# A soft mixture of experts inside a fused kernel: four places for the dispatch weights, the fourth part's maxima earlier, phi loaded by blocks

## The chip, the cores and the metric

The kernel runs on one core of a Trainium2 chip. The time is the device time of that core in microseconds for one run of the whole program; the median over runs is compared. The profile is one execution recorded by the hardware profiler; its times are counted from the start of its span.

## What is computed

The program is a chain of four blocks of attention and feed-forward layers on 16 sequences of 256 tokens with 128 features. The change lies in the feed-forward layer of the second block, a soft mixture of 64 experts with 32 slots each:

```
def _L1_ffn_ref(x, phi, W, b):            # x (16, 256, 128), phi (128, 64, 32), W (64, 128, 128)
    logits = einsum('bmd,dnp->bmnp', x, phi)
    dispatch = softmax(logits, axis=0)     # over the 16 sequences
    combine = softmax(logits.reshape(b, m, n * p), axis=-1)   # over the 2048 slots
    slots = einsum('bmd,bmnp->bnpd', x, dispatch)
    y = einsum('bnpd,nde->bnpe', slots, W) + b[None, :, None, :]
    out = einsum('bnpd,bmnp->bmd', y, combine)
...
x = x + layernorm(_L1_ffn_ref(layernorm(x), ...))
```

The dispatch weights are normalised over the sequences, so each needs the maximum and the sum over all 16 of them; the combine weights are normalised over the slots, which the kernel does with a running maximum.

## The kernel before

The work of the layer is in `stage_soft_moe`. The 2048 slots are cut into eight blocks of 256 slots. For block n three generators are woven together, step by step: `share(n)`, `logits(n + 2)` and `slots(n + 1)`. So a block of the loop finishes the outputs of one block of slots, computes the slot inputs and experts of the next, and the logits of the one after.

- `logits(n)` multiplies, for each of 16 batches b, the transposed tokens by 256 columns of `phi` (L1078) into a bank of `ps_s`. ScalarE copies the bank to `lg` (L1079) and VectorE reduces its maximum into `mpart` (L1080). At the end come the new running maximum and the factors `mfade` and `mless` (L1084 to L1090).
- `slots(n)` works in four parts (c, t): two groups c of 128 slots and two halves t of the 256 tokens. They are called first (0,0), second (0,1), third (1,0) and fourth (1,1). `maxima(c, t)` takes the maximum of `lg` over the 16 sequences (L1101 to L1104), subtracts it (L1105) and has ScalarE take the exponential (L1106), in a tile `mdisp` of 8 KB per partition. `weights(c, t)` sums over the sequences (L1111 to L1115), inverts (L1117) and multiplies (L1118). `inputs(c, half)` multiplies tokens and dispatch weights for eight sequences, into the two `ps_mm` banks, copied to `slT` (L1130); it needs both parts t of its c. `experts(c, half, slT)` adds biases and multiplies by the expert weights `mw`, and ScalarE copies the result to `y`, tile `my` (L1150).
- `share(n)` takes, batch by batch, the exponential of `lg` (L1199), transposes it on TensorE (L1204) into `ps_t`, has it copied to `meT` (L1206), multiplies by `y` into `ps_o`, adds that on VectorE into `x` with the factor `mfade` (L1215; a copy, L1217, for n = 0) and copies the sums of weights to `mgot` on ScalarE (L1218).

`mdisp` has three places that are taken in turn. A part's maxima can start only when the part three before it has been read by `inputs`. `slT` has three places too, and serves `inputs`, the early norm in `late` and the reloaded rows `back` in `end`. PSUM has two banks each for `ps_mm`, `ps_s`, `ps_o` and `ps_t`.

Nothing in this stage is ordered by hand beyond the steps of the generators: the framework's scheduler reorders the instructions of each engine when it builds the program, and each engine then runs its queue in that fixed order. Loads are issued from SP. `phi`, 8 KB per partition, is loaded whole with the tile `quarter` in the pool `soft` at the start of the program (L2009), and its transfer is issued at 40.5 us.

Of the kernel before, what the change touches and what calls it, by code (L numbers as in the profile page):

```python
# [21 lines left out]
F32 = mybir.dt.float32  # L22
# [7 lines left out]
NB, SEQ, P, D = 16, 256, 128, 128  # L30
NG, NT, GT = 8, 4, 512
# [160 lines left out]
def bc(ap, axis, n):  # L192

    ap = ap.unsqueeze(axis)
    shape = list(ap.shape)
    shape[axis] = n
    return ap.to_broadcast(shape)
# [826 lines left out]
def stage_soft_moe(k, x, w, wdram, bdram, xn, xs, fill):  # L1024
# [3 lines left out]

    nc, v = k.nc, k.nc.vector
    ident = k.c["ident"]  # L1030
    phi = w["phi"]
    blocks, bs = 8, 2 * P
    sums = k.t([P, 2, NB], "sums", 1)
    xT = {}
    tile_of = lambda b, t: (b // 2, 2 * (b % 2) + t)
# [3 lines left out]
    y = k.t([P, 2, NB, D + 1], "my", 1)  # L1039
# [4 lines left out]
    quarter = k.t([P, P], "mquarter", 1, dt=BF16)  # L1044
# [3 lines left out]
    def biases():  # L1048


        left = k.t([P, 16 * D], "mdisp", 3)
        nc.gpsimd.memset(left, 0.0)
        for i in range(3):
            nc.sync.dma_start(out=left[32 * i : 32 * i + 4, :], in_=bdram)
        nc.gpsimd.tensor_copy(bias, left)
        for i in (1, 2):
            for at in (slice(32, 64), slice(64, P))[i - 1 :]:
                nc.gpsimd.tensor_tensor(left[at, :], left[at, :], bias[at, :], ALU.subtract)
                nc.gpsimd.tensor_copy(bias[at, :], left[at, :])

    def late(g):

        y = k.t([P, NT, D], "slT", 3)
        yield from k.norm_to(y, xn[g])
        nc.gpsimd.tensor_tensor(x[g], x[g], y, ALU.add)
        yield
        yield from fill(g)

    def logits(n):
        lg = lgs[n % 2]  # L1070
        part = k.t([P, 2, NB], "mpart", 2)
        for b in range(NB):
            if n == 0 and b % 2 == 0:
                xT[b // 2] = k.transposed(xn[b // 2], f"mxT{b // 2}", 1)
            ps = k.ps("s").rearrange("p (t n) -> p t n", t=2)
            for t in range(2):
                g, at = tile_of(b, t)
                k.mm(ps[:, t, :], xT[g][:, at * P : (at + 1) * P], phi[:, n * bs : (n + 1) * bs])  # L1078
            nc.scalar.copy(lg[:, :, b, :], ps)  # L1079
            v.tensor_reduce(part[:, :, b], ps, AX.X, ALU.max)  # L1080
            yield

        new = k.t([P, 2, NB], "mtop", 4)
        v.tensor_tensor(new, top[-1], part, ALU.max)  # L1084
        f = fade[n] = k.t([P, 2, NB], "mfade", 3)
        v.tensor_tensor(f, top[-1], new, ALU.subtract)
        nc.scalar.activation(f, f, AF.Exp)
        top.append(new)
        less[n] = k.t([P, 2, NB], "mless", 3)
        v.tensor_scalar(less[n], new, -1.0, None, ALU.mult)  # L1090

    def slots(n):

        lg = lgs[n % 2]
        disp, rest = {}, []

        def maxima(c, t):
            src = lg[:, t, :, c * P : (c + 1) * P]
            e = disp[c, t] = k.t([P, NB, P], "mdisp", 3)
            m = k.t([P, P], "mm", 1)  # L1100
            v.tensor_tensor(e[:, 0:8, :], src[:, 0:8, :], src[:, 8:16, :], ALU.max)  # L1101
            v.tensor_tensor(e[:, 0:4, :], e[:, 0:4, :], e[:, 4:8, :], ALU.max)
            v.tensor_tensor(e[:, 0:2, :], e[:, 0:2, :], e[:, 2:4, :], ALU.max)
            v.tensor_tensor(m, e[:, 0, :], e[:, 1, :], ALU.max)  # L1104
            v.tensor_tensor(e, src, bc(m, 1, NB), ALU.subtract)  # L1105
            nc.scalar.activation(e, e, AF.Exp)  # L1106

        def weights(c, t):
            e = disp[c, t]
            s = k.t([P, 4, P], "msum", 1)  # L1110
            v.tensor_tensor(s, e[:, 0:4, :], e[:, 4:8, :], ALU.add)  # L1111
            for i in (8, 12):
                v.tensor_tensor(s, s, e[:, i : i + 4, :], ALU.add)
            for i in (2, 1):
                v.tensor_tensor(s[:, 0:i, :], s[:, 0:i, :], s[:, i : 2 * i, :], ALU.add)  # L1115
            r = k.t([P, P], "mrec", 1)
            v.reciprocal(r, s[:, 0, :])  # L1117
            v.tensor_tensor(e, e, bc(r, 1, NB), ALU.mult)  # L1118

        def inputs(c, half):  # L1120

            out = k.t([P, 8, P], "slT", 3)
            for q in range(2):
                ps = k.ps("mm").rearrange("p (b n) -> p b n", b=4)
                for i in range(4):
                    b = 8 * half + 4 * q + i
                    for t in range(2):
                        g, at = tile_of(b, t)
                        k.mm(ps[:, i, :], xn[g][:, at, :], disp[c, t][:, b, :], t == 0, t == 1)
                nc.scalar.copy(out[:, 4 * q : 4 * q + 4, :], ps)  # L1130
            return out

        def experts(c, half, slT):

            pss = [k.ps("mm") for _ in range(2)]
            at = (2 * n + c) * D
            for ps in pss:
                k.mm(ps, quarter, bc(bias[:, at : at + D], 1, 4), True, False)
            for q, ps in enumerate(pss):
                for i in range(4):  # L1140
                    for e in range(4):
                        k.mm(
                            ps[32 * e : 32 * e + 32, i * P : (i + 1) * P],
                            slT[:, 4 * q + i, 32 * e : 32 * e + 32],
                            wc[c][:, e, :],
                            False,
                            True,
                        )
                b = 8 * half + 4 * q
                nc.scalar.copy(y[:, c, b : b + 4, 0:D], ps.rearrange("p (b n) -> p b n", b=4))  # L1150

        wc = []
        for c in range(2):
            at = 2 * n + c
            wc.append(k.t([P, 4, D], "mw", 2))
            nc.sync.dma_start(out=wc[c].rearrange("p n d -> p (n d)"), in_=wdram[:, at * 512 : (at + 1) * 512])
        maxima(0, 0)
        yield
        maxima(0, 1)
        yield  # L1160
        weights(0, 0)
        yield
        maxima(1, 0)
        yield
        weights(0, 1)
        yield
        yield
        yield
        a = inputs(0, 0)
        yield  # L1170
        b = inputs(0, 1)
        yield
        weights(1, 0)
        yield
        maxima(1, 1)
        yield
        experts(0, 0, a)
        yield
        weights(1, 1)
        yield  # L1180
        yield
        a = inputs(1, 0)
        yield
        experts(1, 0, a)
        yield
        experts(0, 1, b)
        yield
        b = inputs(1, 1)
        yield
        experts(1, 1, b)  # L1190
# [37 lines left out]
    def end(g, f, got):  # L1228


        bs = slice(2 * g, 2 * g + 2)
        r = k.t([P, 2, 2], "mend", 3)
        v.tensor_tensor(r, sums[:, :, bs], f[:, :, bs], ALU.mult)
        v.tensor_tensor(r, r, got[:, :, bs], ALU.add)
        rt = k.over[g] if g in k.over else k.t([P, NT], "mendt", 3)
        v.reciprocal(rt.rearrange("p (b t) -> p t b", b=2), r)
        if g in k.over:
            return
        back = k.t([P, NT, D], "slT", 3)
        yield from soft_end(k, x[g], xs[:, g], rt, back)  # L1240
        yield
        if g == 0:
            k.stats_nb(x[g], k.kept)
# [691 lines left out]
def program(ctx: ExitStack, tc: tile.TileContext, xin, dram, at, out):  # L1935
    nc = tc.nc
# [4 lines left out]
    def opened(name, side):  # L1941
        weights[name] = pool(name, side)
        return weights[name].__enter__()
# [4 lines left out]
    def load(p, name, only=None, dt=F32):  # L1948

        got = {}  # L1950
        for n, (a, width) in at[name].items():
            if only is not None and n not in only:
                continue
            src = dram[name][:, a : a + width]
            t = p.tile([src.shape[0], width], dt, tag=f"{name}_{n}", name=f"{name}_{n}")
            nc.sync.dma_start(out=t, in_=src)
            got[n] = t
        return got
# [20 lines left out]
    k = Ctx(tc, const, None, None)  # L1979
# [26 lines left out]
    closed("w0")  # L2006
    l2 = load(opened("wb", "right"), "l2")
    psoft = opened("soft", "right")
    l1f = load(psoft, "l1f")  # L2009
    xs, xn, fill = soft_inputs(k, x, psoft)  # L2010
    stage("l1a", "left", stage_l1_attn, l1, rows1, z, fill, xn, *hand, banks=RING_BANKS)
    closed("z")
    closed("wa")

    stage("l1f", "left", stage_soft_moe, l1f, dram["l1fw"], dram["l1fb"], xn, xs, fill)
    closed("soft")
    pe = opened("we", "right")
# [50 lines left out]
```

## Time and profile before

| | |
|---|---|
| three runs | 2961.12, 2963.91 and 2964.82 us; median 2963.91 |
| the profiled execution | 2960.44 us, of which its span is 2958.7 |
| TensorE clock granted | 0.968 over the span |
| the layer | about 945 to 1535 us |
| `sums` updates (L1223, L1226) | 1099.8, 1165.28, 1230.52, 1295.76 ... 1482.3 |
| matmuls on phi columns (x512) | 141.8 us busy |
| matmuls of `meT` and `my` (x1024) | 144.1 us busy |
| matmuls of `mdisp` and `mxn` (x1024) | 125.3 us busy |
| L1105, L1118 (x32 each) | 73.1 us busy each, 2284 and 2286 ns |
| L1106 (x32) | 61.2 us busy, 1913 ns |

Busy times of one group merge the overlap of matmuls in flight, so the spacing of starts in the timeline is the better measure of what a group costs. A matmul of 32-bit floats counts as two instructions in the profile. In a line of the timeline, the first number is the start, the second the length, and `[1.98 <-ACT mdisp L1106]` says that the engine sat idle for 1.98 us until that instruction of another engine ended. A line of the table of windows gives the window, its length, and for TensorE, its weight loads, VectorE, ScalarE and POOL the busy time and the number of instructions.

### The profile page before, as it was taken

Reading aid. Unit: us, or ns where it says so; the run is one execution under the profiler, and the core shown is the slowest. Engines: PE = TensorE matmul, PEld = TensorE weight load, DVE = VectorE, ACT = ScalarE, POOL = GpSimd, SP = SyncE. Lnnn points to the kernel's source line nnn. Section 1 sums busy time; section 2 is a strip of 40 time slices with the busy share of each in tenths; the row PEclk is TensorE's granted clock in tenths of the full one; section 3 lists DMA queues with packets and bytes.
Section 4 is the critical chain, followed back from the end, with each engine's and each line's share of the span. In section 5 each row is a group of like instructions: output and inputs, shape, how many; then the busy total and the mean of one; then the engine's idle time right before and its main releaser. Section 6 shows DMA issues by size and latency. Waiting matters only on the chain.

```text
span 2958.7 us, 59454 instructions
## 1 busy us (share of the span) xinstructions
PE 2757.9 (93%) x23674; PEld 1878.8 (63%) x23674; DVE 1931.3 (65%) x5302; ACT 1676.9 (57%) x3530; POOL 1017.2 (34%) x1407
## 2 busy tenths in 40 slices
PE   8989999999998799999988998799999799978998
PEld 4556776777766588888863443566666444436897
DVE  5677466565666889999967765666574587735442
ACT  6745656455465676777735666444434377756543
POOL 3553333333336200000044555423221466644332
PEclk9989999999999899999988999899999899998999
DMA  4000000000001000000020000000000000010000
GB/s 116 12 1 2 1 2 2 1 2 1 2 2 38 1 12 12 8 9 8 9 71 5 1 1 1 1 1 1 1 1 1 1 1 1 1 51 7 2 16 16
DMA packets 29150, 31.30 MB, mean 11 GB/s; under 512 B 7292, under 2 KB 20156, under 8 KB 28732
## 3 DMA queue, kind: packets, MB, share of 16 engines
q1 hardware_dynamic: 28872, 27.49, 3.1%
q8 instruction: 187, 3.06, 0.4%
q14 instruction: 91, 0.75, 0.1%
HBM read 23.29 MB, written 4.19 MB: 9 GB/s over the span
## 4 chain that ended last, share of the span: by engine, by line
PE 50%; ACT 7%; DVE 7%; POOL 2%; issue 2%; DMA 0%; POOLq 0%; SPq 0%; ACTq 0%; DVEq 0%
PE ps_s L336 31%; PE ps_o L336 7%; PE ps_mm L336 6%; ACT at_e L491 1%; PE ps_s L325 1%; ACT lg L1199 1%; PE ps_xin L336 1%; ACT meT L1206 1%; PE ps_sum L336 1%; ACT mdisp L1106 1%; ACT lg L1079 1%; PE ps_t L1204 1%; DVE at_nm L459 1%; PE ps_s L525 1%; DVE scan L1488 1%
## 5 line engine op out<-in xcount | busy, mean ns | idle before, releaser
L459 DVE TENSOR_REDUCE at_nm<-ps_s 128x2 f32<-128x512 f32 (+1 forms) x384 | 238.1, 682 | 119.7 <-PE ps_s L336 119.7
L491 ACT ACTIVATE at_e<-ps_s 128x512 f32<-128x512 f32 x384 | 198.2, 603 | 96.7 <-PE ps_s L336 94.6
L1488 DVE TENSOR_TENSOR scan<-ps_s,lm 128x384 f32<-128x384 f32 x256 | 124.7, 549 | 142.4 <-PE ps_s L336 142.2
L497 POOL TENSOR_SCALAR_AFFINE_SELECT at_e<-at_e 128x1024 f32<-128x1024 f32 (+1 forms) x96 | 135.1, 1408 | 208.1 <-ACT at_e L491 207.8
L245 POOL TENSOR_TENSOR ln_rs<-ln_rs,mhalf 128x4 f32<-128x4 f32 x192 | 196.6, 1024 | 15.2
L1015 POOL TENSOR_TENSOR ln_rs<-ln_mv,mendt 128x4 f32<-128x4 f32 x6 | 1.2, 199 | 521.2 <-DVE ln_mv L1013 521.2
L891 DVE TENSOR_REDUCE l_max<-ps_s 128x3 f32<-128x384 f32 x256 | 124.1, 548 | 61.5 <-PE ps_s L336 61.5
L336 PE MATMUL ps_o<-my,meT 128*128 128x129 f32 x1024 | 144.1, 288 | 20.8 <-ACT mgot L1218 16.5
L336 PEld LDWEIGHTS ps_s<-l_w,mlp_h 128*128 128x128 f32 x1280 | 149.7, 192 | 20.3 <-issue 15.1
L336 PE MATMUL ps_s<-l1f_phi,mxT 128*128 128x256 f32 x512 | 141.8, 401 | 21.5 <-DVE mpart L1080 15.7
L244 POOL TENSOR_SCALAR ln_rs<-ln_mv 128x4 f32<-128x4 f32 x184 | 38.5, 209 | 338.0 <-DVE ln_mv L257 317.3
L336 PEld LDWEIGHTS ps_o<-my,meT 128*128 128x128 f32 x1024 | 127.8, 195 | 39.3 <-ACT mgot L1218 22.2
L336 PE MATMUL ps_s<-l_w,mlp_h 128*128 128x128 f32 x1280 | 151.0, 275 | 1.3 <-ACT mlp_h L824 0.9
L336 PE MATMUL ps_s<-qm,kT 32*128 32x512 f32 x768 | 144.4, 650 | 8.0 <-DVE at_nm L459 7.8
L336 PE MATMUL ps_s<-km,qT 32*128 32x512 f32 x768 | 138.4, 666 | 8.7 <-DVE qT L1632 3.7
L941 POOL TENSOR_SCALAR_AFFINE_SELECT e<-e 128x512 f32<-128x512 f32 x128 | 78.6, 635 | 172.8 <-ACT e L938 172.8
L336 PE MATMUL ps_o<-at_e,at_vm 128*32 128x128 f32 (+1 forms) x2048 | 122.7, 336 | 15.3 <-ACT at_oT L521 15.3
L336 PE MATMUL ps_mm<-mdisp,mxn 128*128 128x128 f32 x1024 | 125.3, 279 | 5.0 <-DVE mdisp L1118 4.9
L938 ACT ACTIVATE e<-ps_s 128x384 f32<-128x384 f32 x256 | 105.4, 510 | 39.4 <-PE ps_s L336 39.4
L1465 ACT COPY BT<-ps_s 128x512 f32<-128x512 f32 x64 | 37.6, 587 | 158.0 <-PE ps_s L336 158.0
L336 PEld LDWEIGHTS ps_mm<-mdisp,mxn 128*128 128x128 f32 x1024 | 121.8, 195 | 7.9 <-DVE mdisp L1118 6.6
L336 PEld LDWEIGHTS <-b_ident 128*128 128x128 bf16 x656 | 51.9, 99 | 113.1 <-issue 102.5
(462 smaller groups left out, 7203.1 us busy)
## 6 DMA issues: line engine op xcount, KB each, us to landing
mw<-in_l1fw SPq DMA_DIRECT2D x16, 256.0 KB, 2.6
moe_w<-in_moe SPq DMA_DIRECT2D x16, 256.0 KB, 5.4
l_w<-in_l SPq DMA_DIRECT2D x10, 256.0 KB, 3.3
x<-in_x SPq DMA_DIRECT2D x8, 256.0 KB, 5.8
xs<-x SPq DMA_DIRECT2D x8, 256.0 KB, 2.1
out<-x SPq DMA_DIRECT2D x8, 256.0 KB, 2.5
slT<-xs SPq DMA_DIRECT2D x6, 256.0 KB, 2.7
l1f_phi<-in_l1f SPq DMA_DIRECT2D x1, 1024.0 KB, 5.0
```

What stands on the lines that cost most here:

```text
L244: g.tensor_scalar(out, in_, scale, eps, ALU.mult, ALU.add)
L245: g.tensor_tensor(out, out, self.mhalf[:, :n], ALU.pow)
L325: self.nc.tensor.transpose(out[:n, k * P : (k + 1) * P], src[:, k, cols], self.c["ident"])
L336: self.nc.tensor.matmul(out, lhsT=lhsT, rhs=rhs, start=start, stop=stop, skip_group_check=True)
L459: v_.tensor_reduce(nm[:, t, r, vs], s, AX.X, ALU.max, negate=True)
L491: nc.scalar.activation(e[:, r], s, AF.Exp)
L497: nc.gpsimd.affine_select(at, at, [[0, 4], [0, n], [1, P]], ALU.is_ge, 0.0, base=0, channel_multiplier=-1)
L891: v.tensor_reduce(mx[:, b, :, h, 16], s, AX.X, ALU.max, negate=True)
L938: nc.scalar.activation(e[:, h].rearrange("p j n -> p (j n)"), s[:, : 3 * P], AF.Exp)
L941: nc.gpsimd.affine_select(e[:, :, j, :], e[:, :, j, :], [[0, 4], [1, P]], ALU.is_ge, 0.0, base=0, channel_multiplier=-1)
L1465: nc.scalar.copy(s, ps)
L1488: v.tensor_tensor(m, s[:, : SEQ + P], lm[:, SCAN_HEADS[4 * (t // 2) + 2 * i + hh], :], ALU.mult)
```

## The change

`mdisp` gets four places, so every part takes the place that the same part of the previous block has left. `slT` gets two. In `slots`, the step `maxima(1, 1)` moves from behind `weights(1, 0)` to the step after `weights(0, 1)`, ahead of `inputs(0, 0)`. `phi` is no longer loaded whole: the first 256 columns are loaded at the start into `phi0`, and `logits(n)` issues on SP the load of the 256 columns for `logits(n + 1)` into `mphi`, which has two places. The pool on the right side shrinks by 7 KB per partition and the work pool on the left grows by 6 KB.

```
-    phi = w["phi"]
+    phis = [w["phi0"]]
...
-        left = k.t([P, 16 * D], "mdisp", 3)
+        left = k.t([P, 16 * D], "mdisp", 4)
...
-        y = k.t([P, NT, D], "slT", 3)
+        y = k.t([P, NT, D], "slT", 2)
...
     def logits(n):
         lg = lgs[n % 2]
+        phi = phis[n]
+        if n + 1 < blocks:
+            phis.append(k.t([P, bs], "mphi", 2))
+            nc.sync.dma_start(out=phis[-1], in_=w["phi"][:, (n + 1) * bs : (n + 2) * bs])
...
-                k.mm(ps[:, t, :], xT[g][:, at * P : (at + 1) * P], phi[:, n * bs : (n + 1) * bs])
+                k.mm(ps[:, t, :], xT[g][:, at * P : (at + 1) * P], phi)
...
-            e = disp[c, t] = k.t([P, NB, P], "mdisp", 3)
+            e = disp[c, t] = k.t([P, NB, P], "mdisp", 4)
...
-            out = k.t([P, 8, P], "slT", 3)
+            out = k.t([P, 8, P], "slT", 2)
...
         weights(0, 1)
         yield
+        maxima(1, 1)
         yield
         yield
         a = inputs(0, 0)
         yield
         b = inputs(0, 1)
         yield
         weights(1, 0)
-        yield
-        maxima(1, 1)
         yield
         experts(0, 0, a)
...
-        back = k.t([P, NT, D], "slT", 3)
+        back = k.t([P, NT, D], "slT", 2)
...
-    l1f = load(psoft, "l1f")
+    l1f = load(psoft, "l1f", {"quarter"})
+    a, width = at["l1f"]["phi"]
+    l1f["phi"] = dram["l1f"][:, a : a + width]
+    l1f["phi0"] = psoft.tile([P, 2 * P], F32, tag="phi0", name="phi0")
+    nc.sync.dma_start(out=l1f["phi0"], in_=l1f["phi"][:, : 2 * P])
```

In the instruction order of the changed kernel only this stage differs. From block n=2 to n=5 the order repeats, as it does before. There VectorE starts each block with the maxima of the first and second part interleaved, then the third's; it runs L1101 to L1103 of the fourth part between the steps of the second part's weights, ahead of that part's L1118. TensorE issues `inputs(1, 0)` and `experts(1, 0)` ahead of batch 15's products on `y`, and after them `experts(0, 1)`, `inputs(1, 1)` and `experts(1, 1)`. Before, all of these but the first four matmuls of `inputs(1, 0)` come after batch 15.

## The prediction

> **What bounds the kernel now.** I read the page's busy shares first, then the table of windows over the soft mixture (945 to 1540 us), then the timelines of VectorE and TensorE through one repeating block of it.
>
> ```profile
> PE 2757.9 (93%) x23674; PEld 1878.8 (63%) x23674; DVE 1931.3 (65%) x5302; ACT 1676.9 (57%) x3530; POOL 1017.2 (34%) x1407
> ```
> ```profile
> 1165.00:1230.50 65.50, 63.29 (x652) 55.41 (x652) 59.67 (x101) 47.89 (x104) 0.00 (x0) 1.00 0.03 9
> 1230.50:1296.00 65.50, 63.30 (x653) 55.41 (x652) 59.92 (x103) 47.90 (x103) 0.00 (x0) 1.00 0.03 10
> ```
> The last shows one block: TensorE 63.3 us busy of 65.5, VectorE 59.9, ScalarE 47.9. TensorE is the bound, with VectorE close behind. The line of `sums` (L1226) starts at 1165.28, 1230.52 and 1295.76, so a block takes 65.24 us; blocks n=1 to 5 repeat one order.
>
> VectorE in that block (start, duration, what it waited for):
> ```profile
> 1230.63 1.22 DVE L1101 TENSOR_TENSOR mdisp<-lg 128x1024 f32<-128x1024 f32 x1
> ...
> 1237.81 0.69 DVE L1111 TENSOR_TENSOR msum<-mdisp 128x512 f32<-128x512 f32 x1 [1.98 <-ACT mdisp L1106]
> ...
> 1264.43 2.28 DVE L1118 TENSOR_TENSOR mdisp<-mdisp,mrec 128x2048 f32<-128x2048 f32 x1
> ...
> 1276.93 1.22 DVE L1101 TENSOR_TENSOR mdisp<-lg 128x1024 f32<-128x1024 f32 x1
> ...
> 1291.36 2.29 DVE L1118 TENSOR_TENSOR mdisp<-mdisp,mrec 128x2048 f32<-128x2048 f32 x1
> ...
> 1295.87 1.22 DVE L1101 TENSOR_TENSOR mdisp<-lg 128x1024 f32<-128x1024 f32 x1
> ```
> First part's maxima; the wait for its exponential; the second part's weights, ready at 1266.71; the fourth part's maxima; its weights; the next block. TensorE:
> ```profile
> 1260.08 0.66 PE L1204 MATMUL ps_t<-const_ident,lg 128*128 128x128 f32 x4 [0.29 <-ACT meT L1206]
> 1261.94 2.05 PE L336 MATMUL ps_o<-my,meT 128*128 128x129 f32 x16 [1.21 <-ACT mgot L1218]
> ...
> 1267.46 3.29 PE L336 MATMUL ps_mm<-mdisp,mxn 128*128 128x128 f32 x28
> ...
> 1280.30 0.59 PE L336 MATMUL ps_mm<-mbias,mquarter 128*128 128x512 bf16 x2
> ...
> 1291.42 1.16 PE L336 MATMUL ps_o<-my,meT 128*128 128x129 f32 x8
> ```
> `inputs(0,0)` needs parts one and two; TensorE reaches it at 1267.46, 0.75 us after they are ready, without waiting. So VectorE's road to the second part's weights and TensorE's other work are nearly balanced. That balance is what the change disturbs.
>
> [...] The 1.98 us wait agrees in part: it repeats, but on VectorE, since the second part's place is still held by the previous block. [...] in the trace every block of n=2 to 5 runs the same fixed order, whatever waits. [...]
> ```profile
> 1036.29 5.02 PE L336 MATMUL ps_mm<-mdisp,mxn 128*128 128x128 f32 x28 [3.46 <-DVE mdisp L1118]
> ```
> Next start 1041.15, so 28 matmuls took 4.86 us; at 1267.46 as many took 3.13.
>
> **The change, part by part.** No arithmetic is added or removed: TensorE, VectorE and ScalarE issue the same instructions in a new order, within the soft mixture alone; POOL does nothing in these blocks.
>
> *Costs at nothing.* The 1024 KB phi load becomes eight of 128 KB. A 256 KB `mw` load lands in 2.6 us; each piece has a whole 65 us block. On SP it sits beside the two `mw` loads, and its place was freed when the block before last finished. If the first piece is late, logits(1) starts late: at most about 3 us, more likely 0, since 30 us lie between. `slT` with two places: the third `back` load waits for the first final add (1504.0 plus 1.3 us, 2.7 to land: 1508), needed at about 1515; cover 7 us, cost 0, else up to 6. The layout of memory moves by some KB; at the stage's edges I allow 2 us either way.
>
> *The steady block.* Count from T, the end of batch 15's `ps_o` products, the point where VectorE's queue turns to the next block.
>
> Before: T is 1227.18. The second part is ready at 1266.71, T+39.5, and from there to the next T (1292.42) is 25.7. Sum 65.2.
>
> After, in the instruction order of the changed kernel, VectorE's work from the turn to the second part's L1118, by start-to-start times of this trace: maxima of parts one to three, 3 x 4.48 (1.14+0.60+0.34+0.20+2.20) = 13.4; fourth part's L1101 to L1103, now ahead, 2.1; two sets of weights, 2 x 5.41 (3 x 0.60+0.34+0.20+0.87+2.20) = 10.8; six L1080 x 0.60 = 3.6; six batches of L1215 x 0.52 = 3.1; small ones 0.4. Sum 33.4. The turn comes 1.0 after T (before 3.5: VectorE still had fourth-part weights then). It waits 0.8 on TensorE around batches 2 and 3 (0 to 1.9). Ready at T+35.2: **4.3 earlier**. The 1.98 wait goes, since parts one and two now start together.
>
> But from there the road is longer. The rest of the fourth part's maxima follow at once (0.20+0.26+2.20), then its exponential on ScalarE (1.9), which stands ahead of `mgot` of batch 6, whose bank batch 8's products need: 4.9 us in all against 3.1 us of `inputs(0,0)` matmuls. A new stall of 1.7. Then TensorE's queue to the next T: eight batches of `ps_o` products 7.3; eight phi products 8 x 0.87 = 7.0; `inputs(0,1)` and `inputs(1,0)` 2 x 3.57 = 7.1; `experts(0,0)` and `experts(1,0)` 2 x 2.41 (1280.30 to 1282.71) = 4.8; four sets of transposes 1.8. Sum 28.0. Before, most of `inputs(1,0)` and `experts(1,0)`, 6 us, lay after T, where they filled TensorE while VectorE prepared the second part. Now they lie before T; after T only `experts(0,1)`, `inputs(1,1)` and `experts(1,1)` are left, 8.8. So TensorE comes to `inputs(0,0)` at about T+31.5 and waits about 3.8 for the weights.
>
> Block: 35.2+4.9+28.0 = 68.1, so +2.9, taken as **+3.0**; between +2.0 (no VectorE wait: 34.4) and +5.4 (its waits at 1.9, `experts` at the 2.84 of 1242.55 to 1245.40, and a few tenths for PSUM banks). Five blocks: **+15** (10 to 27).
>
> *Start.* The fourth part no longer waits for `inputs(0,0)` to free a place, so its weights end at about 1029 where they end at 1036. But logits(1)'s last reductions fall behind, with phi(15) at 1037.8 after `inputs(1,0)` and `experts(1,0)`. That is block 0's T. Its T+68 ends at 1105.5, against 1096.85 now: **+8.6** (4 to 12).
>
> *Last slots block (n=6), no logits.* Second part ready at about T+32; 4.4 through the exponential; 22.2 of TensorE work; 1.5 wait for the fourth part's weights: 60, against 56.2 now (1422.9 to 1479.1): **+3.8** (0 to 6).
>
> *End.* All `y` are ready about 8 us after the last T where they take 17.4 (1479.1 to 1496.5): **-9.5** (-11 to -6). After that the ends of the batches run as before.
>
> Sum: 8.6+15+3.8-9.5 = **+17.9**. Against the profiled run (2960.4, span 2958.7 and 1.7 around it) that is 2978.3; the median of the runs is 3.5 above, so 2982. About 0.2%, 6 us, is what a measurement here can tell from no change.
>
> **Rivals.**
> 1. *The fourth place pays (faster).* TensorE's block is 13.9 of phi, 15.8 of `ps_o` products with their turnover, 7.0 of transposes, 14.3 of `inputs` and 11.4 of `experts`: 62.4, so 2.8 of it is waiting. If VectorE is ready by the time TensorE arrives at `inputs(0,0)`, no new wait comes and the old ones may go: 6 blocks x 2.8 = -17, and the start's 7 us earlier weights are kept in part: about 2945. For it: the 1.98 wait, and the 2.45 and 0.78 waits in the first block. Against: the moved 6 us. It decides if the second part is ready before T+31. Chance 0.19.
> 2. *It cancels.* The end's gain of 9.5 against blocks at only +1: 2964. Chance 0.11.
> 3. *The clock drops too.* The new 3.8 us wait before `inputs(0,0)` slows the 28 matmuls behind it as at 1036.29: 1.7 x 6 = +10 more, 2992. For: the line above. Against: that stretch was also sparse before the wait. Chance 0.20.
> 4. *The forecast.* 2982, its own range 2970 to 2993. Chance 0.50.
>
> That the change misses its aim is in the forecast: it sets the fourth part's maxima ahead of the third's weights, but they also come ahead of the second's last multiply.
>
> **How the numbers follow.** Slower: 4 and 3, 0.70; same 0.11; faster 0.19. Range 2957 to 3003: from the weak end of rival 1 to rival 3 with blocks at +4.
>
> **What would show it.** Right: L1226 about 68 us apart; a wait of 3 to 4 us on DVE L1118 before each `inputs(0,0)`; one of 1 to 2 us on ACT `mgot` after it; no 1.98 us wait at the block's start; VectorE's idle up by 3. Wrong: blocks at 65 or less with no L1118 wait. L1118's release under T+32 would sink the main step; waits on DMA or at the stage's edges the ones at nothing.

## The result and the profile after

The change makes the kernel slower by a little: 2981.11 us (median of four runs, 2979.37 to 2981.66) against 2962.51 (2958.86 to 2964.82), a ratio of 1.0064 with a 95% interval of 1.0051 to 1.0077. That lies 0.9 us from the forecast of 2982. The profiled execution took 2981.66 us, its span is 2979.9.

The page's busy line, the first one to read:

```profile
PE 2761.3 (93%) x23674; PEld 1888.3 (63%) x23674; DVE 1925.6 (65%) x5302; ACT 1675.7 (56%) x3530; POOL 1016.7 (34%) x1407
```

The instruction counts are those of before, and busy times moved by at most 6 us (9.5 for the weight loads). So the 21 us between the two profiled executions (spans of 2979.9 and 2958.7 us) are idle time and slower matmuls, not work. The table of windows over two blocks of the layer (window, length, then busy time of TensorE, weight loads, VectorE, ScalarE, POOL; TensorE's clock; DMA):

```profile
1236.17:1304.42 68.25, 63.73 (x651) 56.25 (x650) 58.98 (x102) 47.47 (x101) 0.00 (x0) 0.97 0.04 11
1304.42:1372.66 68.24, 63.72 (x651) 56.24 (x650) 58.97 (x101) 47.47 (x101) 0.00 (x0) 0.97 0.04 11
```

A block takes 68.25 us instead of 65.24. TensorE's clock in it was 1.00 and is now 0.97. VectorE's idle time per block rose from 5.6 us (65.24 less 59.67) to 9.3. The timeline says where. VectorE in one block:

```profile
1236.17 0.69 DVE L1084 TENSOR_REDUCE mpart<-ps_s 128x2 f32<-128x512 f32 x1 [3.51 <-ACT lg L1083]
...
1240.96 0.69 DVE L1084 TENSOR_REDUCE mpart<-ps_s 128x2 f32<-128x512 f32 x1 [3.59 <-ACT lg L1083]
...
1242.18 1.22 DVE L1105 TENSOR_TENSOR mdisp<-lg 128x1024 f32<-128x1024 f32 x1
...
1270.77 1.21 DVE L1105 TENSOR_TENSOR mdisp<-lg 128x1024 f32<-128x1024 f32 x1
...
1273.85 2.27 DVE L1122 TENSOR_TENSOR mdisp<-mdisp,mrec 128x2048 f32<-128x2048 f32 x1
...
1276.50 2.27 DVE L1109 TENSOR_TENSOR mdisp<-lg,mm 128x2048 f32<-128x2048 f32 x1
```

The first two lines are idle time just ahead of the block's turn: VectorE has 7.1 us with nothing to do, because the last two batches' products on phi, which ScalarE copies to `lg` and VectorE reduces (L1084), stand behind `inputs(1,0)` and `experts(1,0)` in TensorE's queue. Then the maxima start (1242.18), the fourth part's come in between (1270.77), and the second part's weights end at 1276.12. TensorE and ScalarE in the same block:

```profile
1240.17 1.16 PE L336 MATMUL ps_o<-my,meT 128*128 128x129 f32 x8
...
1276.17 5.02 PE L336 MATMUL ps_mm<-mdisp,mxn 128*128 128x128 f32 x28 [3.16 <-DVE mdisp L1122]
1281.03 1.06 PE L336 MATMUL ps_o<-my,meT 128*128 128x129 f32 x8
...
1308.42 1.16 PE L336 MATMUL ps_o<-my,meT 128*128 128x129 f32 x8
```
```profile
1278.81 1.91 ACT L1110 ACTIVATE mdisp<-mdisp 128x2048 f32<-128x2048 f32 x1 [1.58 <-DVE mdisp L1109]
1280.62 0.20 ACT L1221 COPY mgot<-ps_o 128x2 f32<-128x2 f32 x2
```

TensorE waits 3.16 us for the weights. Then 28 matmuls take 4.86 us (start of the first to 1281.03), where before they took 3.13. The exponential and `mgot`, which the next `ps_o` products also need, are done at about 1280.8, at nearly the same moment.

### The profile page after: what moved, and what is told of

Read it like the earlier page. It is cut to its first block, busy times and chain, and to the rows that moved or that the text cites. A ratio compares the mean times of both kernels' runs of the same rounds, so it can differ in the third digit from the quotient of the medians.

```text
span 2979.9 us, 59519 instructions
## 1 busy us (share of the span) xinstructions
PE 2761.3 (93%) x23674; PEld 1888.3 (63%) x23674; DVE 1925.6 (65%) x5302; ACT 1675.7 (56%) x3530; POOL 1016.7 (34%) x1407
## 3 DMA queue, kind: packets, MB, share of 16 engines
q8 instruction: 187, 3.06, 0.4%
## 4 chain that ended last, share of the span: by engine, by line
PE 51%; DVE 10%; ACT 4%; POOL 2%; issue 1%; POOLq 0%; ACTq 0%; DVEq 0%
PE ps_s L336 31%; PE ps_o L336 7%; PE ps_mm L336 7%; ACT at_e L491 1%; PE ps_s L325 1%; DVE mdisp L1122 1%; PE ps_xin L336 1%; PE ps_sum L336 1%; DVE mdisp L1109 1%; PE ps_t L1207 1%; DVE mpart L1084 1%; DVE at_nm L459 1%; PE ps_s L525 1%; DVE mdisp L1105 1%; DVE scan L1491 1%
## 5 line engine op out<-in xcount | busy, mean ns | idle before, releaser
L336 PE MATMUL ps_mm<-mdisp,mxn 128*128 128x128 f32 x1024 | 138.5, 297 | 28.3 <-DVE mdisp L1122 28.3
L336 PEld LDWEIGHTS ps_mm<-mdisp,mxn 128*128 128x128 f32 x1024 | 133.6, 211 | 33.2 <-DVE mdisp L1122 30.9
L336 PE MATMUL ps_s<-mphi,mxT 128*128 128x256 f32 x448 | 122.3, 396 | 19.7 <-DVE mpart L1084 19.4
L1084 DVE TENSOR_REDUCE mpart<-ps_s 128x2 f32<-128x512 f32 x128 | 87.3, 683 | 67.0 <-ACT lg L1083 66.8
```

Source lines behind the costliest of these rows:

```text
L336: self.nc.tensor.matmul(out, lhsT=lhsT, rhs=rhs, start=start, stop=stop, skip_group_check=True)
```

## Experiments

The main theory: the layer's order alone makes the difference, through two waits, TensorE's on the second part's weights and VectorE's on the last batches. The rivals: the loads and the smaller `slT`, the four places as such, and the clock. The change consists of four separable things: loads with two `slT` places, the fourth `mdisp` place, the maxima ahead, and a step that goes out of `slots` (one `yield` fewer behind `weights(1, 0)`, so all from `experts(0,0)` on comes a step earlier).

All edits are shown against the changed kernel, unless another is named.

**loads_only.** Three places and the old steps, with the new loads and two places for `slT`:
```
-        left = k.t([P, 16 * D], "mdisp", 4)
+        left = k.t([P, 16 * D], "mdisp", 3)
...
-            e = disp[c, t] = k.t([P, NB, P], "mdisp", 4)
+            e = disp[c, t] = k.t([P, NB, P], "mdisp", 3)
...
-        maxima(1, 1)
         yield
         yield
         a = inputs(0, 0)
...
         weights(1, 0)
         yield
+        maxima(1, 1)
+        yield
         experts(0, 0, a)
```


> The kernel before (three places, the old step order) with only phi's columns loaded a block ahead and slT at two places. Main theory (the loss is all in the order of the instructions): every engine keeps its order, so no difference, 2962 within 4. Rival (the loads or the two slT places cost): part of the change's +18.6 shows here, 2967 to 2981, with waits on DMA or on slT.

Measured 2958.74 us, ratio 0.999 (0.9982 to 0.9998), blocks of 65.18 us. The loads and `slT` cost nothing.

**places_only.** The same with four places.

> The changed kernel with maxima(1,1) put back to its old step, so four places and the loads without the move. Main theory (the move makes the loss, not the places): VectorE's work up to the second part's weights falls to about 31 + 1.8 us after T, TensorE's queue ahead of inputs(0,0) grows to about 32 + 2, so the 3.2 us wait before inputs(0,0) is gone, the block is 63 to 65 us and the time 2945 to 2962. Rival (four places alone upset the order): 2975 to 2985, as the change.

Measured 2937.73 us, ratio 0.9923 (0.991 to 0.9935). It beats both kernels; the time is lower than I expected. The window of one block, and TensorE's line at `inputs(0,0)`:
```profile
1282.58:1346.10 63.52, 61.94 (x620) 54.06 (x616) 60.38 (x107) 46.87 (x102) 0.00 (x0) 1.00 0.04 10
```
```profile
1316.23 6.86 PE L336 MATMUL ps_mm<-mdisp,mxn 128*128 128x128 f32 x60
```
Five blocks take 316.2 us, 63.2 each on average (59.75 to 65.46), the clock is 1.00, and `inputs(0,0)` waits for nothing. One term of my expectation was off: VectorE's weights are ready at 1315.31, 34.7 us after T (1280.62), not 33. They come hardly earlier than in the change (T+35.0). What differs is TensorE, which gets there 0.9 us later than the weights, with more useful work done. What the fourth place frees shows in VectorE's waits for an exponential, from 1110 to 1440 us (engine, line, releaser: total, times, longest), before and here:
```profile
DVE msum L1111 <- ACT mdisp L1106: 12.5, 10, 2.0
```
```profile
DVE msum L1115 <- ACT mdisp L1110: 0.2, 1, 0.2
```

**step_back.** The change with the step put back:
```
         weights(1, 0)
         yield
+        yield
         experts(0, 0, a)
```


> The changed kernel with one empty step put back after weights(1,0), where the change took a step out: maxima(1,1) stays ahead, but experts(0,0) and all that follows is a step later again, so TensorE has about 2.6 us more work after T and ahead of inputs(0,0). Main theory (TensorE's queue arrives too early, and the step taken out is what emptied it): wait before inputs(0,0) from 3.2 to under 1.5, block 64 to 66.5 (from 68.25), time about 2968 (2960 to 2975). Rival (only the fourth part's maxima ahead of the second's last multiply costs): the block stays at 68, 2978 to 2984.

Measured 2959.82 us, ratio 0.999 (0.9983 to 0.9996), blocks of 64.98 us: the time is just under the expected range, the block and the wait are in it. The wait is 0.85 us, with the clock at 1.00:
```profile
1331.92 4.06 PE L336 MATMUL ps_mm<-mdisp,mxn 128*128 128x128 f32 x34 [0.85 <-DVE mdisp L1122]
```

**weights_first.** `step_back` with the second part's weights ahead of the third part's maxima:
```
-        maxima(1, 0)
-        yield
         weights(0, 1)
         yield
+        maxima(1, 0)
+        yield
         maxima(1, 1)
```


> step_back, and weights(0,1) ahead of maxima(1,0). VectorE reaches the second part's weights without the fourth part's first maxima steps, 2.1 us earlier, at about T+32.5; TensorE's queue ahead of the bulk of inputs(0,0) is 29 to 31. Main theory: wait of 0 to 2 us, block 63.5 to 65.5, time 2950 to 2966, under step_back's. Rival (the wait is not set by VectorE's order): as step_back.

Measured 2959.69 us, blocks of 65.18 us, a wait of 1.4 us. All three are in the expected ranges, but the time does not get under that of `step_back`, as the main theory said it would. VectorE was indeed earlier: the weights are ready at T+32.1 instead of T+35.7. But the scheduler also rearranged TensorE's queue, so that it comes to them at T+30.8 instead of T+34.8, with as much more left to do behind them. Earlier weights were worth nothing here, where TensorE's work moved along with them.

**step_out.** `places_only` with the step taken out, the fourth corner:
```
         weights(1, 0)
-        yield
         maxima(1, 1)
         yield
         experts(0, 0, a)
```


> Fourth corner: four places, maxima(1,1) at its old place, but the step between it and weights(1,0) taken out, so that experts(0,0) and what follows is a step earlier, as in the change. If step and move add up (each about +22): 2959. Main theory (both feed one wait: VectorE's work ahead of the second part's weights against TensorE's ahead of inputs(0,0)): VectorE at about 34.5 us, TensorE at about 34, so the wait stays under 1 us and most of the step's cost is hidden: block 64 to 65.5, 2942 to 2953. Rival (the step costs only through TensorE's queue, whatever VectorE does): block 66 or more, 2955 to 2962.

Measured 2958.59 us, ratio 0.999 (0.9983 to 0.9996), blocks of 65.78 us. The number is that of plain addition (2959). My main theory missed: I had counted the two queues up to `inputs(0,0)` and left out what comes before T. The waits of VectorE from 1110 to 1440 us show it:
```profile
DVE x L1218 <- PE ps_o L336: 30.8, 5, 6.2
```
In each block VectorE stands idle for 6.2 us in front of the second half of batch 15's products. TensorE's queue shows what is ahead of them:
```profile
1285.88 0.71 PE L336 MATMUL ps_o<-my,meT 128*128 128x129 f32 x4 [0.59 <-ACT meT L1209]
1286.43 3.29 PE L336 MATMUL ps_mm<-mdisp,mxn 128*128 128x128 f32 x28
1289.56 0.38 PE L336 MATMUL ps_mm<-mbias,mquarter 128*128 128x512 bf16 x1
1289.87 0.62 PE L336 MATMUL ps_mm<-mw,slT 128*32 128x128 f32 x10
1290.42 0.39 PE L336 MATMUL ps_mm<-mbias,mquarter 128*128 128x512 bf16 x1
1290.74 1.73 PE L336 MATMUL ps_mm<-mw,slT 128*32 128x128 f32 x54
1292.40 0.71 PE L336 MATMUL ps_o<-my,meT 128*128 128x129 f32 x4
```
Between the halves of batch 15 stand `inputs(1,0)` and `experts(1,0)`, 6 us of TensorE work. TensorE itself is busy all that time, so its row shows nothing wrong.

**step_out_late and after_late.** To test that reading, the step went back at another point, ahead of `inputs(1,0)` only; `experts(0,0)` stays early. The edit is the same in `step_out` and in the change:
```
         weights(1, 1)
         yield
         yield
+        yield
         a = inputs(1, 0)
```


> step_out with the same empty step ahead of inputs(1,0). In step_out VectorE waits 6.2 us in each block for the last half of batch 15's ps_o products, which stand behind inputs(1,0) and experts(1,0). Here the experts (2.8 us) go behind them, 14 of the inputs' products (3.1 us) stay ahead. Theory 1 (this wait is the whole cost of the step): VectorE's wait falls to about 3.3, block from 65.8 to 63.5 to 64.8, time 2943 to 2953. Theory 2 (the wait is slack and the cost lies in TensorE's waits further on): 2955 to 2961.

> The changed kernel with an empty step put ahead of inputs(1,0) instead of ahead of experts(0,0) as in step_back: experts(0,0) and weights(1,1) stay a step early, only inputs(1,0), experts(1,0) and what follows go back. Theory 1 (the step costs because inputs(1,0) and experts(1,0) stand ahead of the last batches' products, so VectorE sits idle before the next block and TensorE lacks that work after it): as step_back, block 65, wait before inputs(0,0) about 1, VectorE's waits of 3.5 and 3.6 us at the block's end gone, 2957 to 2964. Theory 2 (experts(0,0) a step early is what costs): 2975 to 2984.

Measured: 2945.17 us for the first (0.9948, 0.9934 to 0.9961), blocks of 63.70 us; 2958.38 us for the second (0.9989, 0.9981 to 0.9997), blocks of 65.06 us. Both times and both blocks came out as the first theory says. VectorE's longest wait in the first fell from 6.2 to 3.2 us, as much as was taken out from ahead of batch 15's second half:
```profile
DVE x L1219 <- PE ps_o L336: 17.7, 12, 3.2
```
In the second, one detail of the expectation did not hold: VectorE still has waits of up to 4.0 us on `lg`, 21.7 us in five blocks against 33.6 in the change. With the maxima ahead, the whole cost of the step lies in where `inputs(1,0)` and `experts(1,0)` stand, not in `experts(0,0)`: the time is that of `step_back`. With the maxima at their old place 13.4 of the 20.9 us came back. There the five blocks take 316.9 us, as in `places_only` (316.2); most of the other 7.4 us lies at the start and the end of the layer, and its cause was not looked for.

**fill_wait.** Is the clock part of the loss? The change with products put into the wait:
```
-        def inputs(c, half):
+        def inputs(c, half, r=None):
...
+                        for _ in range(11 if r is not None and (q, i, t) == (0, 0, 1) else 0):
+                            k.mm(ps[:, 3, :], xn[0][:, 0, :], r)
                         k.mm(ps[:, i, :], xn[g][:, at, :], disp[c, t][:, b, :], t == 0, t == 1)
...
-        a = inputs(0, 0)
+        a = inputs(0, 0, r)
```
`r` is the reciprocal that `weights(0, 1)` now returns. Other than the expectation says, the extra products are not without effect: they change part of the result of `inputs(0,0)`.

> The changed kernel with 11 products more in inputs(0,0) (their result is overwritten), which need the second part's reciprocal and so run in the 3.2 us wait ahead of its other matmuls, about 2.5 us of it. TensorE's order else is the same but for three of the inputs' products and one pair of phi products that now come ahead of the ps_o products of the next batch. Theory 1 (the idle 3.2 us costs clock, and the slow matmuls only hide behind the exponential and mgot): the inputs' matmuls run at 0.111 instead of 0.17 us, TensorE's clock in the blocks is 1.00 instead of 0.97, the ps_o products then wait for mgot unless the phi pair covers it, block about 66.6, time 2971 (2967 to 2976). Theory 2 (the matmuls behind the wait are slow for another reason): they stay slow, block 69 or more, 2982 to 2990. Theory 3 (the chain over the exponential alone sets the time, the clock drop is free): 2979 to 2983.

Measured 2971.5 us, ratio 1.0031 (1.0019 to 1.0042): as theory 1 says. TensorE's timeline and a block's window:
```profile
1267.66 2.72 PE L336 MATMUL ps_mm<-mrec,mxn 128*128 128x128 f32 x22 [0.68 <-DVE mrec L1121]
1270.22 3.98 PE L336 MATMUL ps_mm<-mdisp,mxn 128*128 128x128 f32 x34
1274.03 1.03 PE L336 MATMUL ps_s<-mphi,mxT 128*128 128x256 f32 x4
1274.90 1.05 PE L336 MATMUL ps_o<-my,meT 128*128 128x129 f32 x8
```
```profile
1237.27:1304.08 66.81, 64.74 (x678) 56.92 (x674) 58.94 (x102) 47.64 (x102) 0.00 (x0) 1.00 0.04 11
```
22 more instructions on TensorE make each block 1.44 us shorter. The matmuls behind them run at 0.112 us each (34 in 3.81) instead of 0.174 (28 in 4.86). Six more instructions of the inputs and the phi pair, about 1.5 us of work (6 x 0.112 and 0.87), now run ahead of the `ps_o` products in the time that the slow matmuls took. So the 1.44 us come from the full clock and this new order together; neither was tried alone.

**after_inputs.** `places_only` with the fourth part's maxima one step earlier than there (four later than in the change, where the expectation says two), between `inputs(0,1)` and `weights(1,0)`:
```
         b = inputs(0, 1)
         yield
+        maxima(1, 1)
+        yield
         weights(1, 0)
         yield
-        maxima(1, 1)
-        yield
```


> A version that may beat all: four places, the step in, and maxima(1,1) after inputs(0,1) and ahead of weights(1,0), two steps later than the change has it. TensorE's queue ahead of inputs(0,0) is about 34 + 2 us, VectorE's 33 + 1.8: no wait on the second part's weights, no clock drop. Main theory (TensorE is the bound once that wait is gone): block 62.5 to 64.5, 2930 to 2943, so like places_only. Rival (maxima ahead of the third part's weights costs by itself): 2950 or more.

Measured 2940.08 us, ratio 0.9922 (0.9908 to 0.9936), blocks of 62.4 us on average: like `places_only`. Maxima ahead of the third part's weights cost nothing; ahead of `inputs(0,0)` they do.

The four corners with four places, medians in us (the kernel before, run beside each of them, had medians of 2961.89 to 2962.51):

| | step in | step out | difference |
|---|---|---|---|
| maxima at the old place | 2937.73 | 2958.59 | +20.9 |
| maxima ahead | 2959.82 | 2981.11 (the change) | +21.3 |
| difference | +22.1 | +22.5 | |

The fourth place gains 21.0 us (2958.74 to 2937.73), the move loses 22 and the step 21. The change is the sum of one gain and two losses of nearly equal size. The marks of `sums` and `mend` show where they fall. The start is counted from the layer's first product on phi, which the profiled executions reach between 947.66 and 951.14 us, and kernels with the same loads differ by as much:

| | first phi product | from it to the first `sums` | five blocks | to the last `sums` | to the last `mend` |
|---|---|---|---|---|---|
| before | 950.83 | 148.96 | 326.46 | 56.06 | 51.06 |
| places_only | 948.07 | 145.81 | 316.20 | 53.76 | 46.44 |
| step_back | 951.14 | 153.03 | 324.20 | 55.37 | 48.59 |
| step_out | 947.91 | 150.83 | 326.85 | 53.35 | 51.95 |
| the change | 948.48 | 158.60 | 340.99 | 58.36 | 45.72 |

Move and step add up in the total, but not stretch by stretch: the step costs 5.0 us of the start without the move and 5.6 with it, but 10.7 us of the five blocks without and 16.8 with it, and has the opposite sign at the end (+5.5 and -2.9). That the sum is so even is partly chance. Of the move's loss of 22.1 us, 7.2 fall in the start (145.81 to 153.03). There TensorE's bulk of `inputs(0,0)` waits for VectorE, in the change (first line; 7.64 in `step_back`) and in `places_only`:
```profile
1012.12 5.97 PE L336 MATMUL ps_mm<-mdisp,mxn 128*128 128x128 f32 x28 [7.61 <-DVE mdisp L1122]
```
```profile
1011.18 6.96 PE L336 MATMUL ps_mm<-mdisp,mxn 128*128 128x128 f32 x60 [1.06 <-DVE mdisp L1122]
```
The weights come only 0.9 us later, but TensorE has waited 7.6 us with phi products standing behind it in its queue, and then runs 28 matmuls in 5.8 us where 60 took 6.8.

## Why the prediction was right

By its own steps, predicted and measured, in us:

| step | predicted | measured |
|---|---|---|
| second part's weights ready | T+35.2 | T+35.0 (1276.12 less 1241.17) |
| TensorE at `inputs(0,0)` | T+31.5 | T+31.8 |
| its wait | 3.8 | 3.16 |
| from the weights to the next products | 4.9 | 4.9 (1281.03 less 1276.12) |
| the rest of the block | 28.0 | 28.4 |
| block | 68.1 | 68.25 |
| start, from the first phi product | +8.6 | +10.6 (156.57 against 146.02) |
| five blocks | +15 | +14.8 |
| last slots block | +3.8 | +3.3 |
| end | -9.5 | -9.0 |
| sum | +17.9 | +19.7 |

The steady block came out step by step, and that is the part of the forecast that is more than a number. The start cost 2.0 us more than forecast. By the times as they stand, 1105.05 against the 1096.85 that the prediction counts from, it would be +8.2; but the layer's first phi product comes 2.35 us earlier in this execution than in that of the kernel before. From that product to the last `mend` the layer takes 603.67 us against 582.54: 21.1 us more, 1.5 of them behind the last `y`, which the prediction took as equal. The remaining program took 2.4 us longer. It has the same engine orders in both kernels, and over the profiles of this study it varies by about 5 us, so nothing is to be explained there.

The sum of the prediction is thus about 3 us under what the layer costs in the two profiled executions, while the medians differ by 18.6 us. That the forecast of 2982 lies within 0.9 us of the measured median is in part luck: the four runs of the kernel before lie 6 us apart.

- *The stall of 1.7.* The number was right and its named cause was not the active one. I put the inputs' matmuls at 3.1 us and had TensorE then wait for `mgot`. The profile shows no wait of that size: the matmuls themselves take 4.86 us, at a clock of 0.65. Rival 3 saw this clock drop and priced it at 10 us on top. It is not on top, because the exponential's chain of 4.9 covers it: by these times either alone would give nearly the same block. This step hit its number partly by luck. `fill_wait` took the slow matmuls away, and a phi pair came to stand where TensorE would have waited for `mgot`. The other half, a shorter chain over the exponential with the clock still low, was not tried.
- *VectorE's idle time.* "Up by 3" was 3.7. I had seen the 6 us of TensorE work that moved ahead of batch 15 only as work that TensorE then lacks after T. It also starves VectorE ahead of T, by 3.5 and 3.6 us, which the prediction did not name. `step_out` and its late form show what this side costs: 13.4 of 20.9 us where the maxima are at their old place.
- *Costs at nothing.* The phi pieces, `slT` and the layout: `loads_only` confirms them.
- *Rival 1* (the fourth place pays, 2945) did not happen in the change but is real: `places_only` gives 2937.73. The prediction treated its condition, weights ahead of TensorE's arrival, as one question about the whole change. It is met as soon as the edits to the steps are left out, but not as the prediction had it, with the second part ready before T+31: the weights are ready at T+34.7, and TensorE comes at T+35.6.

That a step goes out of `slots` was visible in the diff and in the engine order; the prediction worked from the order and so had its effect, without saying that it was a separate edit with a separate price.

The prediction put VectorE's repeating wait of 1.98 us down to a place that the previous block still holds. `places_only` bears that out: one more place takes 21 us off, and VectorE's waits for the exponential fall from 12.5 us in five blocks to 0.2. That a wait ahead of `inputs(0,0)` slows the matmuls behind it (rival 3) was an estimate from one case, the line at 1036.29. The change shows more of them: in each of the five blocks 3.15 to 3.16 us of recorded wait stand ahead of `inputs(0,0)`, and the 28 matmuls behind it take 4.85 to 4.86 us, at a clock of 0.65. Behind 0.85 us of wait in `step_back` 34 took 3.90 us (1331.92 to 1335.82), and behind 1.37 us in `weights_first` 6 were 0.94 us long, as 6 behind 0.20 us in `fill_wait` were. But the length of the wait does not decide alone. The prediction's case at 1036.29, a wait of 3.46 us with 28 slow matmuls behind it, has a counterpart in `loads_only`, in the same order and with the same wait:
```profile
1033.55 3.39 PE L336 MATMUL ps_mm<-mdisp,mxn 128*128 128x128 f32 x28 [3.46 <-DVE mdisp L1122]
1036.78 0.38 PE L336 MATMUL ps_mm<-mbias,mquarter 128*128 128x512 bf16 x1
```
There the 28 matmuls take 3.23 us; in the kernel before they took 4.86, at a clock of 0.65. Why they were slow in one and not in the other stays open.

## What to carry to other kernels

When a change bundles a buffer with a reordering, price and run each alone: here a gain of 21 us was hidden under two reorderings that lost 43. In a kernel where two engines are nearly balanced, follow an instruction that is moved on both sides: what its engine lacks where it was, and which other engine starves behind it where it now stands. A full row of the bound engine does not show that; the waits of the other engine do.

## What the runs showed of the hardware

Filling an idle stretch with matmuls that the layer does not need made the changed kernel faster, 2971.5 us against 2981.11. With 22 more instructions in the 3.16 us wait, TensorE's clock in the block went from 0.97 to 1.00 and the block from 68.25 to 66.81 us, together with the phi pair that came forward.

Behind the same wait of 3.46 us at the same place, 28 matmuls took 4.86 us in one execution (the kernel before, at a clock of 0.65) and 3.23 us in another (`loads_only`). In the last slots block of the change, 16 `ps_o` products behind a wait of 2.79 us took 3.06 us, at a clock of 0.60, where in the kernel before 16 behind a wait of 2.23 us took 1.89, at 1.00. A wait of 1.74 us ended 6.4 us after that of 2.79: the 28 matmuls behind it took 4.86 us, at 0.65. In `after_late`, 28 matmuls behind a wait of 1.82 us at that place, with no wait above 1.21 us in the 17 us ahead of it, were 3.39 us long in the timeline, against 5.02.
